# A two-layer SmoothQuant, feed-forward, scan and expert kernel: the first feed-forward steps are woven with the last third of SmoothQuant instead of with the scans

## The chip, the cores and the metric

The kernel runs on one core of a Trainium2 chip. The metric is the device time of one execution in microseconds (us), the median over several runs. The core has five instruction queues that run beside each other, each strictly in its own order: TensorE (PE in the profile, its weight loads PEld), VectorE (DVE), ScalarE (ACT), GpSimd (POOL) and SyncE (SP), which here only issues DMAs. An instruction that waits for a result of another queue holds up everything behind it on its own queue.

## The reference, cut to what matters

`x` is (4, 512, 512): four images of 512 rows. Four residual blocks follow one another:

```
x = x + smooth_quant(layernorm(x))              # int8-like linear, silu gate, second linear; per image
x = x + lut_ffn(layernorm(x))                   # W = lut[idx], 16 values; gate, up (1376x512), down (512x1376)
x = x + scan(ctx, layernorm(x))                 # state = state*exp(dt*A) + dt*u*B;  y = state.C;  y *= silu(z)
x = x + experts(layernorm(x))                   # 32 experts, top 8, 192 wide
```

In the first block each image needs absolute maxima over its own rows and columns, two quantised products and the scales back. In the second block the weight matrices do not arrive as numbers but as indices into a table of 16 values; they are looked up once and are then the same for all images. In the third block, z is the layer-normed x, and the scan itself depends only on `ctx` and weights, not on x: only the gate at its end needs x after the second block. The fourth block routes each token to 8 experts.

## The kernel before, in words

One program is traced for one core. A framework turns the traced instructions into five queues: it takes them in roughly the traced order, but by priority and by its own estimates of when inputs are ready, so an instruction may move past others. The traced order is made by generators that each yield after one step, and by `weave`, which always advances the stream that is least far along its stated length.

The stages:

- **Lookups and SmoothQuant.** `lut_weights` has 27 jobs of 4 steps. Each job reads indices (converted and parked in DRAM by POOL DMAs, L303, read back 4-fold by SP DMAs, L319), compares them with four values on DVE (`oh`, L326) and multiplies one-hots by a small table on PE (`pw`, L332); ACT copies the finished weights (L341) to `wg`, `wu`, `wd`. `smooth_quant` has 26 steps for each of the 4 images. `staggered` starts a new image every 15 rounds. Both streams are woven. Its main tiles: `xn` and `w` (quantised in L157, L162, L167, L171), transposes `pt_q` (L177), the first product `ph` (L216), `a` (L222), the same again for `a` and `dw`, and the output `po`, `o` (L234, L238), added to x by POOL (L239).
- **Memory.** SmoothQuant's buffers lie in the pool `ap` on the left side, the lookups' in `lp` on the right side, next to the weights' pool `wp`. The feed-forward's pool `bp` (right) takes the room of `lp`; the scan's pool `mp` and the routing's pool `rp` (left) take the room of `ap`. So the scan's DMAs can't start before SmoothQuant is done with `ap`.
- **`scan_weights` and `routing_constants`** issue 29 SP DMAs: 8 for scan weights, 21 for routing, of which two clear 4.6 MB each (L582) and 16 clear the tables (L580). The scan's first input `cT` (L428) is behind them on SP.
- **Rounds 0 to 3.** Round b weaves `scan(b)` (69 units) with steps of the feed-forward, and from round 1 on with `route(b-1)`, after `gate(b-1)`. `lut_ffn` is cut into half images of 14 steps: one that layer-norms and transposes (`pt_x`, L358), 11 that make a chunk of the hidden row (`pgu`, L371, 8 products each of two passes, then `g`, `h` on ACT and DVE, L379 to L381) and 2 that make the output (`po_f`, L387, 11 products each). There are 8 half images: 112 steps. Round 0 takes 32 of them, rounds 1 and 2 take 28 each, round 3 the last 24.
- **The scan unit.** `scan` first makes its inputs: `pi` (L433), the convolution `acc`, `u` (L444 to L448), `px` (L454), `pd` (L466), `dt`, `dtu` (L470 to L477). Then come 64 units, two for each broadcast `bc` (SP DMA, L487): `st` = exp on ACT (L490), `dBu` on POOL (L492), the scan on DVE (L493), times C on DVE (`sc`, L495), and the sum on PE (`py`, L496, two passes).
- **After round 3**: `gate(3)` and `route(3)` are woven with the first 8 experts; the experts' pool `ep` takes the room of `wp` and `bp`. Then come the other experts, and two passes that add the sums to x.

Of the kernel before, what the change touches and what calls it, by code (L numbers as in the profile page):

```python
# [28 lines left out]
NB = 4  # L29
# [3 lines left out]
TPB = S // P  # L33
# [4 lines left out]
NIC = -(-INTER // P)  # L38
# [891 lines left out]
def run(steps):  # L930
    for _ in steps:
        pass


def staggered(gens, lag):

    step = 0
    while gens:
        for i, g in enumerate(list(gens)[: 1 + step // lag]):
            if next(g, StopIteration) is StopIteration:  # L940
                gens.remove(g)
                step -= lag
            else:
                yield
        step += 1


def weave(*streams):

    streams = [[0, n, g] for g, n in streams]  # L950
    while streams:
        s = min(streams, key=lambda s: s[0] / s[1])
        s[0] += 1
        if next(s[2], StopIteration) is StopIteration:
            streams.remove(s)


@with_exitstack
def tile_kernel(ctx: ExitStack, tc: tile.TileContext, t: dict):
    k = Kernel(tc, t)  # L960
    k.constants(ctx)
    scan = ExitStack()
    with ExitStack() as early:
        k.banks(early, t=2, m=2, y=2, d=2)
        with ExitStack() as ffn:
            wp = ffn.enter_context(tc.tile_pool(name="wp", bufs=1, side="right"))
            with tc.tile_pool(name="ap", bufs=2) as ap, tc.tile_pool(name="lp", bufs=2, side="right") as lp:
                k.lut_tables(wp, wp)
                sq = staggered([k.smooth_quant(ap, b) for b in range(NB)], 15)
                weave((sq, 30 * NB), (k.lut_weights(lp, k.jobs), 4 * len(k.jobs)))  # L970
            bp = ffn.enter_context(tc.tile_pool(name="bp", bufs=2, side="right"))
            rp = ctx.enter_context(tc.tile_pool(name="rp", bufs=1))
            mp = scan.enter_context(tc.tile_pool(name="mp", bufs=2))
            k.scan_weights(mp)
            k.routing_constants(rp)
            steps = (TPB // 2) * (NIC + 3)
            units = KH + 1 + KH * NST
            routes = TPB + 2 + TPB * TOPK

            ffn_ = chain(*(k.lut_ffn(bp, b) for b in range(NB)))  # L980
            for b in range(NB):
                n = steps + (4 if b == 0 else 0)
                streams = [(k.scan(mp, b), units), (islice(ffn_, n), n)]
                if b:
                    run(k.gate(mp, b - 1))
                    streams.append((k.route(rp, b - 1), routes))
                if b == NB - 1:
                    rows = k.table_rows(rp, "xT", k.tables[0], SLOTS, 0, EARLY, ROOM[0])
                    tok = k.table_sum(rp, rows, 0, EARLY, ROOM[0], "a")
                    at = k.slot_tokens(rp, tok, ROOM[0], "a")  # L990
                weave(*streams)
        ep = ctx.enter_context(tc.tile_pool(name="ep", bufs=2, side="right"))
        k.expert_buffers(ep)
        full, nc = SLOTS // P, tc.nc
        two = [k.sums[j % 2] for j in range(full + 1)]
        first = k.pipeline(k.expert(ep, e, (k.xln[0], *at, 0), e, ROOM[0], two) for e in range(EARLY))
        weave((chain(k.gate(mp, NB - 1), k.route(rp, NB - 1)), KH + routes), (first, 2 * EARLY))
    scan.close()
    k.banks(ctx, t=3, g=5)
    k.gu_tag = "g"  # L1000
    tp = ctx.enter_context(tc.tile_pool(name="tp", bufs=6))
    rows = k.table_rows(ep, "exT", k.tables[0] + k.tables[1], SLOTS, EARLY, NE, SLOTS)
    at = k.slot_tokens(rp, k.table_sum(rp, rows, EARLY, NE, SLOTS, "u"), SLOTS, "u")
    rows = k.table_rows(ep, "exT", k.tables[1], SLOTS, 0, EARLY, ROOM[1])
    at_b = k.slot_tokens(rp, k.table_sum(rp, rows, 0, EARLY, ROOM[1], "b"), ROOM[1], "b")
    k.overflow(rp)
    calls = [(e, at, e - EARLY, SLOTS) for e in range(EARLY, NE)]
    for e in range(EARLY):
        calls.insert(2 * e + 1, (e, at_b, e, ROOM[1]))

    sums = [two] * (len(calls) - 2) + [two[:4] + k.sums[1:], k.sums[1:] * 5]
    late = k.pipeline(
        k.expert(ep, e, (k.xln[1], *at, 0), col, n, s) for (e, at, col, n), s in zip(calls, sums)
    )
    run(islice(late, 2 * len(calls) - 2))
    weave((late, 2), (k.add_sums(tp, 0, False), NT // 2))
    run(k.add_sums(tp, 1, True))
    more = nc.values_load(k.more[0:1, 0:1], min_val=0, max_val=1)
    with tc.If(more):
        k.in_full(rp, ep, tp)  # L1020
# [51 lines left out]
```

## Time and profile before

| | us |
|---|---|
| median of 3 runs | 2130.96 |
| the three runs | 2131.37, 2130.96, 2122.72 |
| the profiled execution's own time | 2123.81 |
| its span, first to last instruction | 2121.9 |
| outside the span | 1.9 |
| PE busy | 1847.6 (87%) |
| DVE busy | 1239.2 (58%) |
| ACT busy | 663.6 (31%) |
| POOL busy | 971.8 (46%) |
| mean granted TensorE clock | 0.938 of full speed |

The shares are over stages with different limits: DVE is nearly always busy until about 1240 us and little used afterwards, where the experts run on PE. A time in a table by stretches is a sum of busy time inside the stretch; "(x...)" is the number of instructions.

### The profile page before, as it was taken

The numbers are of one execution on the slowest core, as the hardware profiler recorded it, in microseconds if no ns is written. First come the engines' busy times: TensorE is split into PE (matmuls) and PEld (weight loads), VectorE is DVE, ScalarE is ACT, GpSimd is POOL, SyncE is SP. The second block draws the span as 40 slices with busy tenths as digits, with TensorE's granted clock in tenths as the row PEclk, the third lists the DMA queues.
The fourth block names the chain that finished last, engine by engine and source line by source line (L and its number), as shares of the span: only waits on it lengthen the run. The fifth ranks groups of instructions, "written<-read, shape, count | busy, mean of one in ns | idle before, by whom it ended". The sixth has DMA issues, their size and how long they took to land.

```text
span 2121.9 us, 23529 instructions
## 1 busy us (share of the span) xinstructions
PE 1847.6 (87%) x8367; PEld 1104.3 (52%) x8377; DVE 1239.2 (58%) x2029; ACT 663.6 (31%) x1251; POOL 971.8 (46%) x841
## 2 busy tenths in 40 slices
PE   4777859998988998898979979779999999999980
PEld 2443437543644655374636545456656566666650
DVE  6788743599988878987899754122222222222241
ACT  1553441433433334333523232112222222222210
POOL 3111001166338742775067756645555555555431
PEclk9899969999999998899999999869999999999995
DMA  8421106045325532452235586558787877777765
GB/s 260 113 98 54 70 8 225 32 129 129 100 62 112 109 84 60 111 107 72 82 71 117 103 226 141 102 144 179 165 171 163 168 174 150 165 158 151 143 129 178
DMA packets 184499, 266.06 MB, mean 125 GB/s; under 512 B 43138, under 2 KB 89698, under 8 KB 184372
## 3 DMA queue, kind: packets, MB, share of 16 engines
q1 hardware_dynamic: 142628, 180.12, 31.0%
q0 software_dynamic: 41744, 84.34, 21.8%
q8 instruction: 68, 1.11, 0.2%
q14 instruction: 59, 0.48, 0.1%
HBM read 203.68 MB, written 69.18 MB: 129 GB/s over the span
## 4 chain that ended last, share of the span: by engine, by line
PE 36%; DMA 9%; DVE 6%; issue 3%; POOL 3%; ACT 1%; SPq 0%; DVEq 0%; POOLq 0%; ACTq 0%
PE pg L841 16%; PE po_e L859 12%; PE pt_g L829 3%; DMA sums<-ey,to 3%; DMA bc<-xdbl 3%; DVE st L493 2%; POOL dBu L492 1%; DMA acc<-sums 1%; POOL table L707 1%; PE pgu L371 1%; DVE sc L495 1%; PE po_f L387 1%; DMA table<-i_tok,to 1%; DMA xg<-xln,tokens 1%; ACT st L490 1%
## 5 line engine op out<-in xcount | busy, mean ns | idle before, releaser
L841 PE MATMUL pg<-exT,egu 128*128 128x288 f32 (+1 forms) x1536 | 397.5, 417 | 0.1
L492 POOL TENSOR_TENSOR dBu<-dtu,bc 128x512 f32<-128x512 f32 x256 | 322.9, 1276 | 150.7 <-DMA bc<-xdbl 100.4
L865 POOL DMA_INDIRECT sums<-ey,to x168 | 260.7, 1552 | 228.4 <-DMA sums<-ey,to 130.5
L841 PEld LDWEIGHTS pg<-exT,egu 128*128 128x128 f32 x1536 | 289.0, 191 | 116.6 <-issue 30.3
L493 DVE TENSOR_TENSOR_SCAN st<-st,dBu 128x512 f32<-128x512 f32 x256 | 308.4, 1222 | 55.8 <-POOL dBu L492 28.8
L859 PE MATMUL po_e<-ed,eh 128*128 128x512 f32 (+1 forms) x672 | 307.5, 605 | 6.9 <-DVE eh L854 3.8
L496 PE MATMUL py<-sc,ident 128*128 128x512 f32 x512 | 267.4, 638 | 47.7 <-DVE sc L495 46.6
L490 ACT ACTIVATE st<-dt,A 128x512 f32<-128x512 f32 x256 | 170.7, 686 | 391.0 <-DVE sc L495 374.2
L816 POOL DMA_INDIRECT xg<-xln,tokens x168 | 163.7, 974 | 162.0 <-PE pt_g L829 107.6
L853 DVE SCALAR_TENSOR_TENSOR eh<-eh,pg 64x288 f32<-64x288 f32 (+3 forms) x128 | 58.9, 460 | 245.3 <-ACT eh L852 245.1
L859 PEld LDWEIGHTS po_e<-ed,eh 128*128 128x128 f32 (+1 forms) x672 | 113.4, 178 | 169.8 <-issue 164.0
L332 PE MATMUL pw<-oh,lut_t 128*32 128x344 bf16 (+1 forms) x2052 | 132.2, 377 | 71.2 <-DVE oh L326 70.8
L371 PE MATMUL pgu<-xT,wg 128*128 128x256 f32 (+1 forms) x704 | 182.3, 396 | 1.4 <-DVE o L238 0.5
L496 PEld LDWEIGHTS py<-sc,ident 128*128 128x128 f32 x512 | 93.8, 198 | 163.8 <-DVE sc L495 113.9
L371 PE MATMUL pgu<-xT,wu 128*128 128x256 f32 (+1 forms) x704 | 178.7, 393 | 0.0
L495 DVE TENSOR_TENSOR sc<-st,bc 128x512 f32<-128x512 f32 x256 | 167.6, 679 | 5.2 <-PE py L496 0.5
L371 PEld LDWEIGHTS pgu<-xT,wg 128*128 128x128 f32 (+1 forms) x704 | 133.9, 195 | 60.4 <-issue 39.9
L862 DVE TENSOR_SCALAR ey<-po_e,gates 128x512 f32<-128x512 f32 x64 | 48.0, 750 | 199.9 <-PE po_e L859 183.0
L387 PE MATMUL po_f<-wd,h 128*128 128x512 f32 (+1 forms) x352 | 163.2, 601 | 0.0
L864 ACT ACTIVATE ey<-po_e,gates 128x512 f32<-128x512 f32 (+1 forms) x104 | 71.3, 685 | 285.5 <-PE po_e L859 203.6
L371 PEld LDWEIGHTS pgu<-xT,wu 128*128 128x128 f32 (+1 forms) x704 | 137.6, 197 | 33.3 <-issue 12.4
L707 POOL DMA_INDIRECT table<-i_tok,to x128 | 126.8, 991 | 34.3 <-issue 24.2
(254 smaller groups left out, 1931.0 us busy)
## 6 DMA issues: line engine op xcount, KB each, us to landing
bc<-xdbl SPq DMA_DIRECT2D x128, 512.0 KB
egu<-in_w_gate SPq DMA_DIRECT2D x40, 384.0 KB
ix<-idx_b SPq DMA_DIRECT2D x16, 688.0 KB
egu<-in_w_up SPq DMA_DIRECT2D x40, 256.0 KB
ed<-in_w_down SPq DMA_DIRECT2D x40, 256.0 KB
sums<-zero SPq DMA_DIRECT2D x2, 4608.0 KB
acc<-sums SPq DMA_DIRECT2D x16, 512.0 KB
xln<-xn_r SPq DMA_DIRECT2D x24, 256.0 KB
```

The lines of the kernel that those rows point to most:

```text
L371: nc.tensor.matmul(pg[:m, j * W : (j + 1) * W], lhsT=w[:, k, c * P : c * P + m], rhs=xT[:, k, :], start=k == 0, stop=k == KH - 1,)
L387: nc.tensor.matmul(po, lhsT=h[:m, c, i * P : (i + 1) * P], rhs=self.wd[:m, c, :], start=c == 0, stop=c == NIC - 1,)
L490: nc.scalar.activation(st, dt[:, e, :], AF.Exp, scale=self.A[:, e, n : n + 1])
L492: nc.gpsimd.tensor_tensor(dBu, dtu[:, e, :], bc[:, 0, :], ALU.mult)
L493: nc.vector.tensor_tensor_scan(st, st, dBu, 0.0, ALU.mult, ALU.add)
L495: nc.vector.tensor_tensor(sc, st, bc[:, 1, :], ALU.mult)
L496: nc.tensor.matmul(py[e], lhsT=self.ident, rhs=sc, start=n == 0, stop=n == NST - 1)
L707: scatter = nc.gpsimd.indirect_dma_start(out=tables[k % len(tables)], out_offset=bass.IndirectOffsetOnAxis(ap=to[:, i, k : k + 1], axis=0) ...
L816: nc.gpsimd.indirect_dma_start(out=xg[:m, :], out_offset=None, in_=xln, in_offset=bass.IndirectOffsetOnAxis(ap=tokens[:m, lo + j, col : co ...
L841: nc.tensor.matmul(pg[i][:, :hs], lhsT=w[:, k, i * P : (i + 1) * P], rhs=xT[:, k, z : z + hs], start=k == 0, stop=k == KH - 1,)
L859: nc.tensor.matmul(po[:m, :], lhsT=h[:, k, b : b + m], rhs=wd[:, k, :], start=k == 0, stop=k == 1)
L865: nc.gpsimd.indirect_dma_start(out=sums[j], out_offset=bass.IndirectOffsetOnAxis(ap=to[:m, lo + j, col : col + 1], axis=0), in_=y[:m, :], ...
```

## The change

The same instructions are traced, in another order. SmoothQuant's generators are made before the lookups, and the first step is taken at once. The lookups are woven with 80 steps of SmoothQuant instead of with all of them (81 of its 104 steps are then traced). `lp` is closed at that point, `bp` takes its room while `ap` is still open, and the rest of SmoothQuant is woven with 24 steps of the feed-forward (one whole half image, then the transposes and 9 chunks of the next). Round 0 takes 28 steps instead of 32, rounds 1 and 2 take 28 as before, and only 4 are left for round 3, which had 24.

```diff
-            with tc.tile_pool(name="ap", bufs=2) as ap, tc.tile_pool(name="lp", bufs=2, side="right") as lp:
+            steps = (TPB // 2) * (NIC + 3)
+            ffn_ = chain.from_iterable(k.lut_ffn(bp, b) for b in range(NB))
+            with tc.tile_pool(name="ap", bufs=2) as ap:
+                sq = staggered([k.smooth_quant(ap, b) for b in range(NB)], 15)
+                next(sq)
                 k.lut_tables(wp, wp)
-                sq = staggered([k.smooth_quant(ap, b) for b in range(NB)], 15)
-                weave((sq, 30 * NB), (k.lut_weights(lp, k.jobs), 4 * len(k.jobs)))
-            bp = ffn.enter_context(tc.tile_pool(name="bp", bufs=2, side="right"))
+                with tc.tile_pool(name="lp", bufs=2, side="right") as lp:
+                    n = 30 * NB * 2 // 3
+                    weave((islice(sq, n), n), (k.lut_weights(lp, k.jobs), 4 * len(k.jobs)))
+                bp = ffn.enter_context(tc.tile_pool(name="bp", bufs=2, side="right"))
+                weave((sq, 30 * NB - n), (islice(ffn_, steps - 4), steps - 4))
             rp = ctx.enter_context(tc.tile_pool(name="rp", bufs=1))
             mp = scan.enter_context(tc.tile_pool(name="mp", bufs=2))
             k.scan_weights(mp)
             k.routing_constants(rp)
-            steps = (TPB // 2) * (NIC + 3)
             units = KH + 1 + KH * NST
             routes = TPB + 2 + TPB * TOPK
-
-            ffn_ = chain(*(k.lut_ffn(bp, b) for b in range(NB)))
             for b in range(NB):
-                n = steps + (4 if b == 0 else 0)
+                n = steps
                 streams = [(k.scan(mp, b), units), (islice(ffn_, n), n)]
```

The framework's queues of the changed program (they are fixed when it is built) show what it makes of this. Counted in products on PE: between the last lookup and the first scan product there were 115 products of the feed-forward and are now 232, of which 118 stand among SmoothQuant's last ones. Round 0, from the first scan product to the first product of the gate, held 153 and now holds 202. Rounds 1 and 2 hold 236 as before. Round 3 held 204, and 24 products of the first experts; it now holds 38, and 54 of the first experts. Before round 3's last scan unit the POOL queue held 11 expert instructions and now holds 24.

## The prediction

> **What bounds the kernel now.** I read the page first, then a table by stretches cut at the stage borders of the timeline, then the PE and SP timelines around the borders, then the waits of the scan rounds. The cuts: 26 first lookup product, 287 last lookup, 377 first scan product (`pi`), 422 first scan unit, 552, 778, 1007 and 1236 the gates of images 0 to 3.
>
> Table by stretches (busy us of PE, PEld, DVE, ACT, POOL, granted clock, DMA share, GB/s):
>
> ```profile
> 26.00:287.00 261.00, 203.79 (x2596) 113.45 (x2603) 206.07 (x324) 118.88 (x187) 41.78 (x41) 0.90 0.31 96
> 287.00:323.00 36.00, 17.40 (x101) 11.25 (x98) 14.12 (x26) 17.18 (x31) 3.81 (x4) 0.72 0.00 0
> 323.00:377.00 54.00, 54.00 (x214) 40.12 (x214) 15.73 (x57) 7.13 (x15) 3.40 (x11) 1.00 0.63 221
> 377.00:422.00 45.00, 42.33 (x131) 24.11 (x129) 26.28 (x36) 22.07 (x31) 6.18 (x4) 0.92 0.12 38
> 422.00:552.00 130.00, 114.92 (x308) 54.46 (x309) 124.78 (x154) 51.26 (x78) 80.10 (x67) 0.97 0.45 117
> 622.00:778.00 156.00, 144.69 (x447) 83.40 (x446) 133.45 (x180) 53.93 (x88) 110.31 (x97) 0.97 0.50 98
> 1007.00:1076.00 69.00, 63.23 (x253) 41.56 (x252) 59.66 (x120) 27.97 (x45) 12.41 (x11) 0.94 0.18 64
> 1076.00:1236.00 160.00, 142.30 (x428) 79.87 (x428) 135.11 (x181) 52.48 (x91) 120.46 (x107) 0.96 0.56 125
> 1236.00:1390.00 154.00, 121.99 (x442) 69.86 (x440) 50.88 (x114) 32.49 (x76) 88.58 (x76) 0.89 0.64 144
> ```
>
> The hole is 287 to 323: SmoothQuant's tail runs alone, PE busy half the time at a clock of 0.72. From 323 to 377 PE is full of feed-forward while the scan's inputs arrive. In round 0's units DVE is busy 124.8 of 130 us: DVE is the limit. In rounds 1 to 3 both are near theirs (PE 145 and DVE 133 of 156).
>
> PE's and SP's timelines at the border (start us, duration):
>
> ```profile
> 283.63 3.71 PE L332 MATMUL pw<-oh,lut_t 128*32 128x512 bf16 x30
> ...
> 360.88 16.48 PE L387 MATMUL po_f<-wd,h 128*128 128x512 f32 x38
> 377.19 7.03 PE L433 MATMUL pi<-cT,in_w 128*128 128x512 f32 x16
> ```
>
> ```profile
> 325.60 0.38 SPq L402 DMA_DIRECT2D in_w<-in_in_w  x1
> ...
> 344.74 11.71 SPq L428 DMA_DIRECT2D cT<-in_ctxT  x1
> ```
>
> The scan's inputs are in at 344.7 + 11.7 = 356.5; `pi` starts only at 377.2, because its place on PE's queue is behind the feed-forward. The start of the scan is set by PE's order, not by the DMAs. That is the fact on which my forecast rests.
>
> Groups (busy us, mean ns):
>
> ```profile
> L493 DVE TENSOR_TENSOR_SCAN st<-st,dBu 128x512 f32<-128x512 f32 x256 | 308.4, 1222 | 55.8 <-POOL dBu L492 28.8 <-ACT st L490 25.3
> L495 DVE TENSOR_TENSOR sc<-st,bc 128x512 f32<-128x512 f32 x256 | 167.6, 679 | 5.2 <-PE py L496 0.5
> L380 DVE SCALAR_TENSOR_TENSOR g<-g,pgu 128x256 f32<-128x256 f32 (+1 forms) x88 | 35.9, 409 | 27.5 <-ACT g L379 27.5
> ```
>
> 64 units need 64 x (1.222 + 0.679) = 122 us of DVE in every round, whatever PE does.
>
> **The change part by part.** It adds and removes no instruction; it moves them.
>
> *End of the lookups.* Out of this stretch go, by the two DVE queues, one `w` multiply (2.29), one `w` maximum (2.28), four `o` (4 x 0.75) and small ones (0.5); four layer-norm instructions (1.7) come in: 6.4 us less DVE work, with PE, ACT alike. DVE is busy 206 of 261 there, so 6.4 / 0.79 = 8 us. Last lookup: 287.4 - 8 = 279. At the start POOL issues one index DMA ahead of the first layer-norm's `ln_rs` instead of six, so five wait for x; it waited until 12 us before, while the first lookup began at 26: the cover is 14 us, cost nothing, between -5 and +5. Bounds for the stretch: -17 (SmoothQuant no longer ends alone) to 0.
>
> *SmoothQuant's tail with the first half image.* PE now has 118 products there: 8 transposes 1.3, 88 of `pgu` (322.8 to 360.9, 38.1), 22 of `po_f` (44 passes at 16.48 / 38 = 0.434, 19.1): 58.5 us. SmoothQuant's own PE work was 17.4 less 2 for transposes of the feed-forward; transposes of `xn` (1.8), one column broadcast (1.2) and four `po` (1.9) come in: 20 us. 78 us of PE, against a SmoothQuant chain that took some 65 us (from the `xn` multiply at 255.6) and can hide under it. I add 4 for the start (`xn` is written after the last lookup's buffers are free) and 4 for waits among the two shared `m` banks: 86. Bounds 80 and 96. The tail ends at 279 + 86 = 365.
>
> Its clock: the table shows 0.72 in the sparse tail and 1.00 in the full stretch after it. The Trainium skill ("TensorE: Matmul & The Clock Gate", section "What's actually happening") says that an idle PE drops to half clock and a busy one is released after some 3.4 us; by it the 20 us would shrink by a quarter, 5 us less. I keep 20.
>
> *The second half image.* 114 products are still ahead of `pi`: 1.3 + 38.1 + 18 x 0.867 = 55 us. `pi` starts at 420 instead of 377: **+43** (25 to 57). The scan's DMAs start when `ap` is free, near 367, and take the same 31 us (325.6 to 356.5): 398, hidden by 22 us of feed-forward. Without that cover each us shows on the scan.
>
> *Round 0.* From `pi` to the first unit, 45 us as before. The units then carry 49 products more, nearly all `pgu`: 49 x 0.432 = 21 us of PE on 115, and 12 DVE instructions (12 x 0.41 = 5) less 1.6 of layer-norm. By DVE alone 130 x 128 / 125 = 133.5; by PE 136 busy, and rounds 1 and 2 took 1.08 us per busy us: 147. Between them, nearer to PE: **+12** (3 to 17). Gate 0 at 607.
>
> *Rounds 1 and 2.* The same numbers of instructions on each queue: **0** (-4 to +4 each).
>
> *Round 3.* 166 products leave. DVE loses 36 feed-forward instructions (36 x 0.41 = 15) and gains 10 of the experts (5). Before the first unit little changes: -3. In the units DVE keeps 135 - 12 + 5 = 128, POOL gets 13 expert instructions of about 1 us on 120: 133. At round 0's share (96%) DVE takes 133, at the present share (84%) 152; POOL can't be under 133, and the first experts' weights now load beside the broadcasts `bc`. 140, so -20; together **-23** (-8 to -31).
>
> The wait that goes, and what is late next, in round 3's units:
>
> ```profile
> ACT st L490 <- DVE sc L495: 95.7, 33, 9.9
> PEld py L496 <- DVE sc L495: 24.4, 27, 3.3
> POOL dBu L492 <- DMA bc<-xdbl: 17.7, 13, 4.1
> ```
>
> ACT's and PE's waits on DVE show who leads; POOL's wait for `bc` stays.
>
> A rule that speaks against the change: "Perfetto Trace Analysis", section "Identifying the Most-Contended Engine", judges TensorE by the busy share of weight loads. In round 0's units that is 54.5 of 130, 42%, beside DVE's 96%: by the rule PE has room, DVE is the engine to feed, and putting PE work ahead of it gives only DVE's +3.5 in round 0 and nothing from PE in round 3 (-10): the sum would be +43 + 3.5 - 10 - 8 = +28. The same page (section "Optimization Strategy") recommends interleaving regimes, which is what the change does.
>
> *After round 3.* 30 products of the first experts, one expert's worth (13.9 us, the distance of two experts' first `po_e` on PE's timeline, 1291.7 and 1305.6), are done earlier. They stood between those of `gate(3)` and `route(3)` (5.3 us of `po_e` ahead of the last gate transposes alone); that chain gets shorter. But the products behind the route are the same: **-8** (-14 to 0).
>
> Sum: +43 + 12 + 0 - 23 - 8 = **+24** on 2123.8 (span 2121.9 and 1.9 around it), 2148. The median of the runs shown, 2131, lies 7 above the profiled time; I put the new median at **2150**, between the two bases.
>
> **The rivals.** *PE is the path all the way (faster).* Then only PE's holes count: 287 to 323 loses 18.6 us of idle, and the delay of the scan is paid back in full, since rounds 0 to 3 have 117 products of the feed-forward, some 55 us, less. That both are near 90% in rounds 1 to 3 is for it, DVE's 96% in round 0 against it. By the low ends of my terms: +25 for `pi`, +3 for round 0, -31 for round 3, -14 after it: -17, 2107 on the profiled time and 2114 on the median. It decides from the point where round 3 and what follows it give back 11 us more than `pi` and round 0 lose: at best 45, so the two may lose 34 at most, and `pi` must start before 408. 0.17.
>
> *The two ends cancel (no change).* With terms between mine and those, `pi` +33, round 0 +8, round 3 -28, after it -10: +3, 2127 to 2134. 0.22.
>
> *The weave holds SmoothQuant up (slower still).* PE puts 8 products between SmoothQuant's pieces; if its ten or so links (product, DVE, ACT, product) each wait for 2.5 us of them more than assumed, the tail takes 25 more, `pi` starts at 445 and the sum is +49: 2172 to 2180. It is the upper part of my slower case, which has 0.61 in all.
>
> 0.5%, 10.7 us, is about what a measurement of this kernel can tell from no change. The range 2112 to 2178 takes in the case of no change, the near end of the faster one and all but the far end of the waits.
>
> **What would show it.** Right: last lookup near 279, PE full from there to `pi` near 420, `cT` landed by then; first unit near 465, gate 0 near 607, gates 1 and 2 226 and 229 later, gate 3 some 206 after gate 2, with DVE above 90% there. Wrong: `pi` before 408, or round 3 under 190 us (faster); a PE with gaps in SmoothQuant's tail, or `cT` after its place on PE's queue (slower than forecast).

## The result, and the profile after

| | us |
|---|---|
| median after, 5 runs | 2145.4 (2142.1 to 2146.9) |
| median before beside it, 5 runs | 2123.7 (2120.1 to 2131.4) |
| ratio of the times | 1.0084, 95% interval 1.0063 to 1.0105 |
| the profiled execution after, and its span | 2143.3, 2141.5 |

The changed kernel is slower by 0.8%, and the forecast of 2150 lay 5 us above it. But two of its terms were badly mis-sized and nearly cancelled, so that the total came this close is luck. The experiments below are about those two. First the same views as before.

The table by stretches of the changed kernel (busy us of PE, PEld, DVE, ACT, POOL, granted clock, DMA share, GB/s). The cuts: 256 last lookup, 348 the transposes of the second half image, 403 first scan product, 446 first scan unit, 585 gate 0, 1041 gate 2, 1265 gate 3.

```profile
20.00:256.00 236.00, 190.59 (x2554) 108.84 (x2558) 199.88 (x322) 104.40 (x169) 37.81 (x37) 0.91 0.36 113
256.00:262.00 6.00, 0.42 (x6) 0.00 (x0) 0.36 (x2) 5.61 (x7) 1.27 (x1) 0.81 0.01 3
262.00:348.00 86.00, 77.24 (x341) 54.11 (x347) 30.70 (x61) 27.67 (x50) 9.70 (x9) 0.95 0.00 1
348.00:403.00 55.00, 54.84 (x221) 40.84 (x221) 17.05 (x60) 8.34 (x17) 2.10 (x9) 1.00 0.61 217
446.00:585.00 139.00, 129.26 (x403) 72.31 (x402) 125.85 (x159) 49.34 (x80) 79.17 (x66) 1.00 0.42 110
1041.00:1101.00 60.00, 54.41 (x185) 27.58 (x183) 44.97 (x86) 25.03 (x39) 8.02 (x7) 0.97 0.24 82
1101.00:1265.00 164.00, 109.72 (x220) 39.93 (x220) 142.89 (x181) 53.32 (x89) 136.43 (x121) 0.82 0.64 151
```

Three things are to be seen. The lookups end 31 us earlier than before (256 instead of 287), with PE busy 190.6 us there instead of 203.8. The hole of SmoothQuant's tail is nearly closed: PE is busy for 77 of 86 us, at a clock of 0.95 instead of 0.72. And a new hole has opened at the other end: in the last round (1041 to 1265) PE is idle for 224 - 54.4 - 109.7 = 60 us, where before it was idle for 229 - 63.2 - 142.3 = 23. The round is hardly shorter for it.

PE's timeline of the changed kernel at the borders (start us, duration, and in brackets the idle time before it and what ended it), then SP's:

```profile
255.59 0.83 PE L332 MATMUL pw<-oh,lut_t 128*32 128x512 bf16 x9 [0.54 <-DVE oh L326]
262.45 2.25 PE L358 MATMUL pt_x<-ident,xn 128*128 128x128 f32 x8 [6.03 <-ACT xn L107]
...
387.55 15.62 PE L387 MATMUL po_f<-wd,h 128*128 128x512 f32 x36
403.01 7.03 PE L433 MATMUL pi<-cT,in_w 128*128 128x512 f32 x16
```

```profile
350.68 0.38 SPq L402 DMA_DIRECT2D in_w<-in_in_w  x1
...
369.66 11.34 SPq L428 DMA_DIRECT2D cT<-in_ctxT  x1
```

The first scan product again follows directly on the feed-forward, 22 us after the issue of its input load ended on SP at 381 (the profile does not show when the load landed).

The waits of the last round's units in the changed kernel (us in total, times, longest us):

```profile
PEld py L496 <- DVE sc L495: 89.9, 56, 7.2
ACT st L490 <- DVE sc L495: 86.0, 49, 7.5
...
DVE st L493 <- POOL dBu L492: 11.2, 12, 2.4
POOL dBu L492 <- DMA bc<-xdbl: 7.4, 6, 2.2
```

PE's weight loads now wait 90 us for DVE there (24 before), DVE waits nearly twice as long for POOL (6.2 before), and POOL's wait for `bc` has fallen from 17.7 to 7.4. This suggests that POOL now helps to set the pace; experiments 2, 10 and 11 test that.

### The profile page after: what moved, and what is told of

Its sections match the earlier page's. It is cut to its first block, busy times and chain, and to the rows that moved or that the text cites. A ratio compares the mean times of both kernels' runs of the same rounds, so it can differ in the third digit from the quotient of the medians.

```text
span 2141.5 us, 23503 instructions
## 1 busy us (share of the span) xinstructions
PE 1859.7 (87%) x8363; PEld 1104.0 (52%) x8377; DVE 1231.9 (58%) x2029; ACT 663.6 (31%) x1251; POOL 974.7 (46%) x841
## 5 line engine op out<-in xcount | busy, mean ns | idle before, releaser
L496 PE MATMUL py<-sc,ident 128*128 128x512 f32 x512 | 284.0, 668 | 87.0 <-DVE sc L495 85.0
L859 PE MATMUL po_e<-ed,eh 128*128 128x512 f32 (+1 forms) x672 | 312.6, 613 | 8.5 <-DVE eh L854 4.1
L371 PE MATMUL pgu<-xT,wg 128*128 128x256 f32 (+1 forms) x704 | 175.5, 388 | 5.0 <-DVE o L238 2.9
L371 PE MATMUL pgu<-xT,wu 128*128 128x256 f32 (+1 forms) x704 | 172.5, 383 | 0.0
L332 PE MATMUL pw<-oh,lut_t 128*32 128x344 bf16 (+1 forms) x2052 | 123.2, 364 | 41.9 <-DVE oh L326 41.7
L371 PEld LDWEIGHTS pgu<-xT,wu 128*128 128x128 f32 (+1 forms) x704 | 133.0, 190 | 29.7 <-issue 10.9
```

The source lines that it names most:

```text
L371: nc.tensor.matmul(pg[:m, j * W : (j + 1) * W], lhsT=w[:, k, c * P : c * P + m], rhs=xT[:, k, :], start=k == 0, stop=k == KH - 1,)
L496: nc.tensor.matmul(py[e], lhsT=self.ident, rhs=sc, start=n == 0, stop=n == NST - 1)
L859: nc.tensor.matmul(po[:m, :], lhsT=h[:, k, b : b + m], rhs=wd[:, k, :], start=k == 0, stop=k == 1)
```

## The experiments

All times are each kernel's median, all ratios against the kernel before on the same chip. The table gives the profiled executions, in us: the start of the first scan product `pi`, the rounds (round 0 from `pi` to gate 0, the others from gate to gate), the stretch behind gate 3, and PE's idle time (stretch less busy) from the start to gate 3.

| kernel | last lookup | `pi` | round 0 | round 1 | round 2 | round 3 | behind gate 3 | PE idle | ratio |
|---|---|---|---|---|---|---|---|---|---|
| before | 287 | 377 | 174 | 226 | 229 | 229 | 886 | 182 | 1 |
| after | 256 | 403 | 182 | 225 | 230 | 224 | 877 | 189 | 1.0084 |
| 1 lookups only | 254 | 368 | 173 | 226 | 229 | 232 | 885 | 186 | 0.9956 |
| 2 experts held | 252 | 399 | 182 | 225 | 228 | 213 | 890 | 199 | 1.0147 |
| 3 inputs first | 256 | 380 | 199 | 226 | 230 | 226 | 870 | 191 | 1.0070 |
| 4 inputs first, 14 steps | 257 | 360 | 182 | 220 | 223 | 216 | 875 | 162 | 0.9836 |
| 5 14 steps | 256 | 402 | 175 | 207 | 224 | 216 | 886 | 169 | 0.9935 |
| 6 before, inputs first | 287 | 333 | 200 | 219 | 224 | 231 | 889 | 168 | 0.9883 |
| 8 inputs first, 32/24/24/18 | 257 | 360 | 194 | 212 | 214 | 219 | 881 | 165 | 0.9811 |
| 9 round 0 emptied | 256 | 402 | 169 | 210 | 228 | 233 | 894 | 184 | 1.0034 |

The gates in this table are marked by the gate's multiplication on DVE (L512). The gate's first transposes on PE follow 3 to 8 us later elsewhere, but 14 to 16 us later at gates 0 to 2 of kernel 4 and at gates 1 and 2 of kernel 5, and 10 and 14 us later at gates 0 and 1 of kernel 8, because PE still has feed-forward products in front of them. PE's timeline of kernel 4, where DVE's multiplication of gate 0 starts at 541.9:

```profile
545.86 1.88 PE L496 MATMUL py<-sc,ident 128*128 128x512 f32 x4
547.58 9.61 PE L387 MATMUL po_f<-wd,h 128*128 128x512 f32 x22
...
557.88 1.04 PE L518 MATMUL pt_y<-ident,u 128*128 128x128 f32 x8
```

Cut at those transposes (called PE's mark below), rounds 0 to 3 take 186, 225, 231 and 224 us in the changed kernel, 198, 220, 221 and 206 in kernel 4, 179, 219, 222 and 206 in kernel 5, and 204, 217, 204 and 218 in kernel 8. For these three kernels what a single round gains depends on the mark; the sums hardly do.

**1. Half of the change: the lookups' split without the feed-forward.**

```diff
-                weave((sq, 30 * NB - n), (islice(ffn_, steps - 4), steps - 4))
+                run(sq)
-                n = steps
+                n = (32, 28, 28, 24)[b]
```

> Half of the change alone: the lookups are woven with 80 steps of SmoothQuant, the rest of SmoothQuant then runs by itself, and the feed-forward stays with the scans in the old shares (32, 28, 28, 24 steps). Theory 'a swap': the lookups end near 256 us as in the changed kernel (31 earlier than before), but only because SmoothQuant's last third was taken out of them; that third alone is a chain of about 65 us (estimate: the tail of the changed kernel took 92 us with 58.5 us of feed-forward products in it, and the old tail 36 us with 132 of 176 products), so it ends near 321 and the first scan product starts at 370 to 380, against 377.2 before. Time within 10 us of the kernel before, 2115 to 2133. Rival 'the lookups themselves got cheaper': the tail takes the old 36 to 45 us, the first scan product starts near 350, and the time is 2092 to 2100. Rounds 0 to 3 take as long as before in both (174, 226, 229, 229).

Measured: 2113.2 us, ratio 0.9956 (0.9939 to 0.9973). The windows of this kernel, lookups and tail:

```profile
20.00:254.00 234.00, 186.94 (x2555) 107.04 (x2556) 197.80 (x318) 104.46 (x169) 37.45 (x37) 0.93 0.36 114
255.00:316.00 61.00, 27.86 (x132) 19.44 (x134) 21.53 (x33) 29.25 (x45) 10.62 (x10) 0.61 0.00 1
```

The lookups end at 254 without any feed-forward beside SmoothQuant, so the 31 us belong to the new split and start of the lookups, not to the weave. But they are mostly a swap: the tail now takes 62 us instead of 36, and `pi` comes only 9 us earlier. The time lies 2 us below the range of the swap (2115 to 2133) and 13 above that of the rival. Against this kernel the changed one starts the scan 35 us later: some 58.5 us of feed-forward products (the forecast's price for them) lengthened a tail of 62 us to 92, so about half of them were hidden. The time for the second half image (52 and 55) is nearly the same in both.

**2. The first experts held back.** Three reads keep the weights' memory until the last scan unit:

```diff
+            last = mp.tile([P, 3], F32, name="last", bufs=1)
+            for i, w in enumerate((k.wg, k.wu, k.wd)):
+                nc_ = tc.nc
+                nc_.vector.tensor_tensor(last[:, i : i + 1], w[:, 0, 0:1], k.scanned[:, KH - 1, S - 1 : S], ALU.add)
         ep = ctx.enter_context(tc.tile_pool(name="ep", bufs=2, side="right"))
```

> The changed kernel, with the memory of the weight tables wg, wu, wd held by three one-column reads that need the last scan unit of image 3, so that no load and no gather of the first experts can start before the scan is done. Theory 'the first experts hold the last round up': their 24 instructions on the POOL queue (16 gathers at 1.06 us, 3 scatters, 5 memsets; with the gaps of 0.3 us between them some 28 us) stand between the dBu products, and their weights ahead of bc; without them the last round's units take 135 to 148 us instead of 163.6, and gate 3 comes 15 to 28 us earlier; the stretch behind gate 3 gets longer by 10 to 20 us, because the first experts' start is lost there. Time 2130 to 2145. Rival 'DVE and the routing set the round': the units stay at 158 to 165 us, and the whole gets slower by what is lost behind gate 3, 2150 to 2165.

Measured: 2150.6 us, ratio 1.0147 (1.0119 to 1.0175); the single times spread widely, 2138.9 to 2154.7. The last round's units:

```profile
1096.00:1247.00 151.00, 89.09 (x136) 28.03 (x136) 131.76 (x170) 45.60 (x67) 113.57 (x97) 0.75 0.42 102
```

The units took 151.0 us instead of 163.6: the first experts had cost them 12.6, less than I gave them (15 to 28), and behind gate 3 the 13 us came back (890 against 877). So neither theory holds whole: the experts do hold the round up, but the median is the rival's, and 151 us, with PE idle for 62 of them, is still not the 140 of the forecast. The profiled execution is the fastest of the four; what made the other three 8 to 16 us slower is not shown.

**3 and 4. The scan's input ahead of the routing constants**, with 24 and with 14 steps in the tail:

```diff
+            sc = [k.scan(mp, b) for b in range(NB)]
+            next(sc[0])
             k.routing_constants(rp)
...
-                streams = [(k.scan(mp, b), units), (islice(ffn_, n), n)]
+                streams = [(sc[b], units), (islice(ffn_, n), n)]
```

and for the fourth kernel also:

```diff
-                weave((sq, 30 * NB - n), (islice(ffn_, steps - 4), steps - 4))
+                weave((sq, 30 * NB - n), (islice(ffn_, 14), steps - 4))
-                n = steps
+                n = (28, 28, 28, 14)[b]
```

> The changed kernel, with the first step of scan(0) (its input load cT and its first column) traced before routing_constants, so that 21 loads and clears stand behind cT on SP instead of ahead of it; the queue of PE then has 80 products of the second half image ahead of the first scan product instead of 114. Theory 'PE's queue sets the start of the scan': cT lands before 370, and the first scan product follows SmoothQuant's end (348) by 80 products x 0.43 us + 1.3 = 36 us, so it starts near 383 instead of 403. Some 35 products move into round 0 (15 us of PE beside 97% of DVE): round 0 grows by 5 to 14 us. Time 2145 - 20 + 5 to 14 = 2130 to 2139. Rival 'the loads set it': the place on PE's queue does not matter, cT still lands near 381 because the DMA engines share among the loads, and the first scan product starts at 383 with PE idle before it for over 5 us. Rival 'PE bounds round 0': the round takes back all of the 20 us, time 2142 to 2147.

> As the run before (cT ahead of the routing constants), and the weave with SmoothQuant takes 14 feed-forward steps (one half image) instead of 24; the rounds take 28, 28, 28 and 14 steps. On PE's queue 22 products stand between SmoothQuant's end and the first scan product instead of 114. Theory 'PE's queue sets the start of the scan': the tail ends near 348 as in the changed kernel, cT lands near 360 and the first scan product starts at 360 to 364, 40 us earlier than in the changed kernel; round 0 has about the same products as in the changed kernel (182 us, up to 190), rounds 1 and 2 stay at 225 and 230, the last round gets 10 more feed-forward steps and fewer of the experts (224, +0 to +8). Time 2145 - 40 + 0 to 16 = 2105 to 2121, faster than both kernels or level with the one before. Rival 'PE is the path': the delay of the scan was free, what is brought forward is paid back in the rounds, 2138 to 2147. Rival 'DMA': cT lands near 381 and the time is 2122 to 2130.

Measured: 2135.1 us, ratio 1.0070 (1.0049 to 1.0091), and 2085.0 us, ratio 0.9836 (0.9814 to 0.9857). SP's timeline of the fourth kernel, then PE's:

```profile
355.11 0.43 SPq L428 DMA_DIRECT2D cT<-in_ctxT  x1
```

```profile
358.76 1.03 PE L371 MATMUL pgu<-xT,wu 128*128 128x256 f32 x4
359.62 7.03 PE L433 MATMUL pi<-cT,in_w 128*128 128x512 f32 x16
```

`pi` starts at 380 and 360, where the numbers of products ahead of it on PE's queue put it (383 and 360 to 364), with PE full in front of it. The edit also traces the scan's first column earlier, but up to the first scan product PE's traced order stays the same. In the third kernel round 0 takes back 16.6 of the 23 us, more than the 5 to 14 expected: 34 products of 0.43 us, 15 us of PE, cost their full time beside a DVE that is busy for 131 of 152 us in the units. In the fourth kernel, with the steps spread otherwise, round 0 is 182 as after by the table's mark, and rounds 1 to 3 are 5 to 8 us shorter each; by PE's mark round 0 is 12 us longer than after, and the last round 17 shorter. It beats both kernels, and it lies 20 us below its expected range (2105 to 2121), because rounds 1 and 2 were expected unchanged and the last no shorter.

**5. 14 steps alone**, the inputs as in the changed kernel:

```diff
-                weave((sq, 30 * NB - n), (islice(ffn_, steps - 4), steps - 4))
+                weave((sq, 30 * NB - n), (islice(ffn_, 14), steps - 4))
-                n = steps
+                n = (28, 28, 28, 14)[b]
```

> The changed kernel with 14 feed-forward steps in the weave with SmoothQuant instead of 24, the rounds take 28, 28, 28 and 14; the scan's inputs are loaded as in the changed kernel. On PE's queue 114 products stand between SmoothQuant's end and the first scan product, exactly as in the changed kernel; only the rounds differ. Theory 'start and rounds add up': the first scan product starts at 403 as in the changed kernel, round 0 loses 66 products against it and takes 172 to 176 us, as in the kernel before (174.4), and rounds 1 to 3 take 220, 223 and 216 as in the run with 14 steps and early inputs; span 403 + 174 + 220 + 223 + 216 + 875 = 2111, time 2113 (2105 to 2121). Rival 'PE is the path and the start is free': it is the same work as in that run, 2080 to 2092. Rival 'the early inputs made rounds 1 to 3 shorter, not the steps': these rounds take 225, 230, 224 and the time is 2127 to 2135.

Measured: 2112.3 us, ratio 0.9935 (0.9913 to 0.9958): the sum of start and rounds, 2113, to a us, though not term by term: round 1 took 207 by the table's mark (219 by PE's), not 220, and the stretch behind gate 3 took 886, not 875. With the same `pi` at 402 as the changed kernel it is faster by 1.5%, and faster than the kernel before, so the delayed scan start alone does not make a kernel slower than before; what the rounds get counts as well. And by the ratios the fourth kernel, with the earlier start, is another 1.0% faster, so the start is not free either.

**6. The kernel before, with the inputs first**, the only edit to it:

```diff
             k.scan_weights(mp)
+            sc = [k.scan(mp, b) for b in range(NB)]
+            next(sc[0])
             k.routing_constants(rp)
...
-                streams = [(k.scan(mp, b), units), (islice(ffn_, n), n)]
+                streams = [(sc[b], units), (islice(ffn_, n), n)]
```

> The kernel before, with the scan's first input load ahead of the routing constants as the only edit; 23 products instead of 107 stand between SmoothQuant's end and the first scan product on PE. Theory 'PE's queue sets the start, and round 0 takes two thirds of it back' (as the run of the changed kernel with early inputs showed: 23 earlier, 16.6 longer): the first scan product starts at 334 to 340 instead of 377, round 0 grows from 174 to 195 to 205 us, rounds 1 to 3 as before: 2124 - 40 + 25 = 2109 (2100 to 2116). Rival 'all paid back': round 0 takes 212 or more, 2117 to 2126. Rival 'hardly paid back': round 0 stays under 188, 2085 to 2098.

Measured: 2100.7 us, ratio 0.9883 (0.9859 to 0.9907). `pi` at 333, 45 us earlier; round 0 grew by 26 us, as expected. That would leave 19 us; the kernel gained 25, since rounds 1 and 2, expected unchanged, got 7 and 5 us shorter, and round 3 and the stretch behind it 2 and 3 longer. Why rounds 1 and 2 did is not shown.

**7. SmoothQuant's first step behind the tables again**, one run:

```diff
-                next(sq)
                 k.lut_tables(wp, wp)
+                next(sq)
```

> The changed kernel, with the first step of SmoothQuant taken after the tables of the lookups as before; PE's order behind the lookups is the same. It splits the 31 us by which the lookups end earlier. Theory 'most of it is the work taken out and the better fill, some 7 us the order at the start': the first lookup starts near 26 and the last ends at 262 to 265, and everything behind is 6 to 8 us later. Rival 'the start did nothing': the last lookup ends at 254 to 258 all the same. Rival 'the start did most': it ends at 270 or later.

Measured: 2147.5 us. The first lookup began at 19.1, no later than in the changed kernel (19.7); the last ended at 261, where the other kernels with this split lie between 252 and 257. So the order of the first step is worth some 5 us at most, in a single run, and is not the reason for the earlier first lookup. What the queues show instead: in this kernel two index loads stand on POOL ahead of the first `ln_rs`, in the changed one 1, in the kernel before 6, where the first lookup came at 26.5. That link is argued, not tested.

**8. The fourth kernel with 32, 24, 24 and 18 steps in the rounds:**

```diff
-                n = (28, 28, 28, 14)[b]
+                n = (32, 24, 24, 18)[b]
```

> The run with early inputs and 14 steps, with the rounds taking 32, 24, 24 and 18 steps instead of 28, 28, 28 and 14: some 27 and 34 products leave rounds 1 and 2 (12 and 15 us of PE), 27 go to round 0 and 30 to the last round. Theory 'PE sets rounds 1 and 2, DVE and POOL set rounds 0 and 3': in that run PE was busy 207 of 220 us in round 1, 167 of 182 in round 0 and 177 of 216 in the last; rounds 1 and 2 get 8 to 12 us shorter each, round 0 3 to 12 longer and the last 0 to 6; time 2085 - 20 + 10 = 2075 (2068 to 2082). Rival 'it is one sum of products, wherever they stand': 2083 to 2090. Rival 'DVE's chain of 64 units sets every round': no round changes by over 3 us.

Measured: 2085.7 us, ratio 0.9811 (0.9788 to 0.9833). By the table's mark rounds 1 and 2 got shorter by 8 and 9 us, as expected of rounds that PE sets, round 0 got 12 longer, the last 2.5, and 5.6 came on behind gate 3; by PE's mark it is 3 and 17 shorter, 6 and 12 longer. Either way rounds 1 and 2 together gave 17 to 20 us. The whole is not told apart from the fourth kernel's, since the intervals of the ratios overlap: the rival's total, with the direction of the theory's parts.

**9. Round 0 emptied instead of the last round**, the tail's 24 steps as changed:

```diff
-                n = steps
+                n = (8, 28, 28, 24)[b]
```

> The changed kernel with the 24 steps in the weave with SmoothQuant as they are, but taken out of round 0 instead of the last round: the rounds take 8, 28, 28 and 24 steps instead of 28, 28, 28 and 4. The first scan product starts at 403 as in the changed kernel. Theory 'the last round cannot use the room': without feed-forward the last round still took 224 us, with PE idle for 60 of them against 23 before, since DVE and POOL set it; given its 24 steps back it takes 228 to 233, and PE's idle time there falls to 23 to 32; round 0, which DVE sets too (152 busy of 182), falls to 163 to 170; round 1, with some 30 products less in front of it, takes 210 to 226; behind gate 3 it takes 885 as before. Time 403 + 166 + 220 + 229 + 231 + 885 + 2 = 2136 (2122 to 2142), 5 to 20 less than the changed kernel. Rival 'feed-forward costs the same in every round': round 0 gains what the last round loses, 2140 to 2150.

Measured: 2138.9 us, ratio 1.0034 (1.0017 to 1.0051), 0.5% below the changed kernel's ratio; its interval does not touch that of the changed kernel. Round 0 gave 13 us, round 1 gave 15 and round 2 gave 3; the last round took 9 more and its idle PE fell from 60 to 30 us; behind gate 3 17 came back, where 8 were expected. Feed-forward does not cost the same in every round, but most of what it gave in the first rounds was lost again behind gate 3.

**10 and 11. The last round's units alone.** The tenth kernel is the second with the routing of image 2 traced behind the units:

```diff
-                    streams.append((k.route(rp, b - 1), routes))
+                    if b < NB - 1:
+                        streams.append((k.route(rp, b - 1), routes))
...
+            run(k.route(rp, NB - 2))
```

> The changed kernel with the first experts held until the last scan unit, as in the second run, and with the routing of image 2 (32 scatters on POOL at 1.0 us and 0.3 us between them, some 19 us of DVE) traced behind the last round's units instead of among them. It leaves the 64 scan units of the last round nearly alone. Theory 'routing and experts on POOL and DVE took the place of PE': the units go from 163.6 (changed kernel) and 151 (experts held) to 126 to 134, DVE busy for 92% or more of them; the routing shows up again behind gate 3, by 30 us or more. Rival 'the chain of a unit sets the pace' (ACT, POOL, DVE and their waits, whatever else is queued): they stay at 142 to 152.

Measured, one run: 2165.6 us, units 163.6. The framework put the routing among the units all the same, with its 32 scatters on POOL in one bunch. The windows of the tenth kernel there:

```profile
1176.00:1196.00 20.00, 8.76 (x9) 2.00 (x8) 8.91 (x9) 2.77 (x4) 17.37 (x17) 0.50 0.45 75
1196.00:1216.00 20.00, 11.78 (x12) 3.00 (x12) 10.05 (x12) 4.16 (x6) 16.73 (x17) 0.61 0.38 63
```

POOL is busy for 34 of 40 us, 21.4 of them with 23 of the scatters, 12.7 with 11 `dBu`; the scatters have 6 us of gaps besides. DVE, which waits for its `dBu`, is busy for 19. The eleventh kernel makes the routing wait by data: four one-column additions to image 2's x need the last unit.

```diff
+            for i in range((NB - 2) * TPB, (NB - 1) * TPB):
+                nc_.vector.scalar_tensor_tensor(
+                    k.x[:, i, 0:1], k.scanned[:, KH - 1, S - 1 : S], 0.0, k.x[:, i, 0:1], ALU.mult, ALU.add
+                )
+            run(k.route(rp, NB - 2))
```

> As the run before, which did not do what it should (the framework put the routing of image 2 among the last round's units all the same, its 32 scatters in a bunch at 1176 to 1216 us, where DVE was busy for 19 of 40 us). Here four one-column additions of zero to image 2's x need the last scan unit, so its routing can't start before. It leaves the 64 scan units alone on DVE, POOL and ACT. Theory 'routing and experts on POOL and DVE took the place of PE': the units go from 163.6 (changed kernel) and 151 (experts held) to 124 to 132, DVE busy for 93% or more of them. Rival 'the chain of a unit sets the pace' (ACT, POOL, DVE and their waits, whatever else is queued): they stay at 142 to 152. The time as a whole gets longer by the routing that is now behind the units: 2150 or more.

Measured, one run: 2186.0 us. A window of its last round, and DVE's timeline near the end of it:

```profile
1178.00:1198.00 20.00, 14.18 (x21) 3.47 (x21) 19.03 (x22) 7.03 (x11) 12.93 (x11) 0.83 0.54 135
```

```profile
1218.96 1.22 DVE L493 TENSOR_TENSOR_SCAN st<-st,dBu 128x512 f32<-128x512 f32 x1
1220.29 0.69 DVE L495 TENSOR_TENSOR sc<-st,bc 128x512 f32<-128x512 f32 x1
```

64 units from 1098.0 to 1221.0: 123 us, DVE at 95%, as the theory has it. The gate came only at 1252, because the routing now stood in front of it. From the first scan to the end of the last `sc` the changed kernel needed 163.1 us and the kernel with the experts held 149.1. So the 163 are 123 of DVE's own pace, 26 for the routing among the units, and 14 for the first experts. In both cases most of it is work of DVE itself: DVE was busy for 142.1 us of the 163.1, for 130.7 of the 149.1 and for 116.3 of the 123, so the routing brought DVE 14 us of instructions and 12 of waiting, the experts 11 and 3.

## Why the prediction was right, and where it was wrong

- **The start of the scan hangs on PE's queue: right.** Experiments 3, 4 and 6 moved the order, and `pi` went with it (377 to 333, 403 to 380 and 360), each time with PE full ahead of it. The reason for the order is probably one step further back: the framework estimated `cT` by its place on SP and filled PE until then. That is inferred: up to the first scan product the edit leaves PE's traced order alone and moves SP's, but the estimates themselves were not seen.
- **End of the lookups, -8 (bounds -17 to 0): mis-sized, -31.** I counted the 6.4 us that leave DVE and took PE "alike". PE lost 13 us of busy time as well, the first lookup began 7 us earlier (I had called that free, -5 to +5), and the idle time of PE between the first and the last lookup fell by another 12. Experiment 1 shows that it belongs to the new split and start, not to the weave. How the 12 come about stays open.
- **The tail, 86 (80 to 96): right, 92**, 6 of them a start at which PE waits for `xn`, where I had given 4. PE busy 77 there, forecast 78. The Trainium skill's rule on the clock ("TensorE: Matmul & The Clock Gate", section "What's actually happening") has an idle PE at half clock and a busy one at full clock. Here, alone, SmoothQuant's products kept PE busy for 24.4 us at a granted clock of 0.61 (experiment 1, whose 27.9 us of PE hold 20 passes of feed-forward as well); in the weave they did for 18.4 us at 0.95. That agrees with the rule, by the granted clock and by the durations; I had kept 20 us.
- **Second half image 55: right, 54.8. `cT` hidden by 22 us: right.** `pi` +43 (25 to 57): measured +25.8; the lookups ended 23 us earlier than forecast, and the tail took 6 more. That `cT` had landed is shown only in so far as PE stayed full up to `pi`: what the forecast read as the landing is the end of the load's issue on SP.
- **Round 0 +12 (3 to 17): right, +7.7. Rounds 1 and 2 at 0: right, -1.0 and +1.2.**
- **Round 3, -23 (-8 to -31): mis-sized, -5.0, outside its bounds.** Ahead of the units I took -3, measured -8.2; in the units -20, measured +3.2. Two things failed. DVE's work in the units did not fall from 135 to 128 but rose to 143: part of the routing slid from the stretch ahead of the units (DVE 59.7 to 45.0) into them, some 9 us by the rows of experiment 2, and the experts brought 11 where I had counted 5. And of the two shares that I had, 84% and 96%, I took a time near the second. I had taken PE for what kept DVE below it. Experiments 2 and 11 show that it was the routing's and the experts' instructions on POOL and DVE; DVE's share stayed at 87%, where "above 90%" was my sign of being right. With the present share my own sum gave 152 for the units and, with the -3 ahead of them, -11 for the round.
- **Behind gate 3, -8 (-14 to 0): right, -9.1.** By experiment 2 these belong to the experts' early start.

The sum of the measured steps is 25.8 + 7.7 - 1.0 + 1.2 - 5.0 - 9.1 = 19.6, the difference of the two spans; 23 too little gain at the lookups and 18 too much in the last round made +24 of it.

Of the rivals, "PE is the path all the way" was to decide if `pi` came before 408. It came at 403, and the kernel was still slower, since round 3 and the stretch behind it gave back 14 us and not 45. Cancelling was not reached either. "The weave holds SmoothQuant up" cost 6 us, not 25.

The Trainium skill's rule of the most-contended engine ("Perfetto Trace Analysis", section "Identifying the Most-Contended Engine") gave +28 in all, +3.5 in round 0 and -10 in round 3; measured were 19.6, 7.7 and -5. That its sum is nearer than mine says nothing for it, because the +43 in it is the same mis-sized term. Its premise, PE with room in round 0 because weight loads are at 42%, does not hold here: in experiment 6, the kernel before with more products in that round, PE's busy time there rose from 157 to 190 us and the round grew by 26. In the changed kernel, with weight loads at 52%, experiment 3 put 15 us of products more into it and it grew by 16.6.

As one account: the change closed 32 us of PE's idle time at the start (lookups 83 to 62, tail 19 to 14, round 0 18 to 12) and opened 37 in the last round. So PE's idle time up to gate 3 hardly changed (182 to 189 us), yet gate 3 came 28.7 us later. The other 22 us are PE's busy time ahead of it, which rose from 1054 to 1076: 84 passes of the first experts' products stood there instead of 20, and in the last round, at a granted clock of 0.86 instead of 0.96, a `py` pass took 767 ns instead of 631. Behind gate 3 only 9 us came back.

Experiments 5 and 9, which give the last round feed-forward back with the same tail and the same `pi`, are faster than the changed kernel by 1.5% and 0.5%. That agrees with the account but does not single out the 37 us: in experiment 9 the last round and the stretch behind it lost 26 of the 31 us that rounds 0 to 2 won. Experiments 4 and 5 also have rounds 1 and 2 that are 5 to 9 us shorter than the changed kernel's by PE's mark, with the same products in all of them but round 1 of experiment 5, which has 14 fewer. Why they are shorter is not settled.

## What to carry to other kernels

Work that is moved to fill a hole opens one where it came from; ask of that place which engine will set the pace there, and count every queue's instructions in it, not only the engine that is relieved. When the start of a stage hangs on an engine's order, look for what the scheduler believed about the inputs: one load moved ahead of 21 others was worth 1.2% in the kernel before, and with 14 of the woven steps the kernel was 1.6% faster than before. DVE's busy share in one stretch (96% in round 0) can't be carried over to another where other instructions stand among its own (87% in the last round).

## What the runs showed of the hardware that was not expected

The issue of one 512 KB load lasted 11.3 us on SP behind two clears of 4.6 MB, and 0.43 us ahead of them (changed kernel and experiment 4). With the load ahead it took longer from `pi` to the first unit: 47, 50, 54 and 50 us in experiments 3, 4, 6 and 8, against 43 to 45 in the others, but 48 in experiment 5, which has the load behind. That the clears then fall on the scan's own loads is a guess.

A DVE instruction on one column, which takes 0.14 to 0.16 us where POOL is idle beside it, lasted as long as two POOL products beside it. DVE's and POOL's timelines of the changed kernel:

```profile
1136.39 2.54 DVE L698 TENSOR_TENSOR more_p<-more_p,most 128x1 f32<-128x1 f32 x1
```

```profile
1136.42 2.49 POOL L492 TENSOR_TENSOR dBu<-dtu,bc 128x512 f32<-128x512 f32 x2
```

The Trainium skill ("SBUF — State Buffer", section "SBUF: two separate sides") says that VectorE, in an instruction with two inputs from SBUF, and GpSimd take one shared pair of ports in turn, each for a whole instruction. The lengths of the two rows agree with that, though DVE's row begins 0.03 us ahead of POOL's. The other places of this instruction agree too: in all runs it took 0.14 to 0.16 us where no POOL instruction ran beside it (0.16 at 1308.64 in the changed kernel), and 0.3 to 4.2 us where one did, and then it ended within 0.05 us of a POOL instruction's end (4.23 us beside a `dtu` of 4.52 in experiment 5).
